# The first image's 3x3 convolution in pairs of rows, in a kernel of four layers (conv, scan, attention, filter)

## Chip, cores and metric

The kernel runs on one core of a Trainium2 chip. Its time is the device time of one execution in microseconds (us). The engines are TensorE (PE in the profile; its weight loads are PEld), VectorE (DVE), ScalarE (ACT), GpSimd (POOL) and SyncE (SP), whose queue issues all the DMAs here.

## What is computed

The input is x, four images of 64 x 64 points with 96 channels, in float32. Only the first part of layer 0 matters for the change:

```python
xz = x @ W_in.T                       # after a group norm of x
xp, z = xz[..., :192], xz[..., 192:]
xc = conv_general_dilated(xp, conv_w, (1, 1), [(1, 1), (1, 1)])   # 3x3, 192 -> 192
xc = silu(xc + conv_b)
x_dbl = xc @ x_proj_w.T               # 6 rows for delta, 16 for B, 16 for C
delta = softplus(dts @ dt_proj_w.T + dt_proj_b)
y = selective_scan(xc, delta, A, B, C)   # along rows and along columns, both ways
x = x + (y * silu(z)) @ W_out.T
```

Layer 1 (a depthwise 3x3 and a 1x1 convolution), layer 2 (linear attention and a quantised feed-forward) and layer 3 (an FFT filter and a second feed-forward) follow. They and the scans are the same text in both kernels.

## The kernel before

**Tiling.** Channels lie on partitions, points along the free dimension. An image is 4096 points, cut into 8 blocks (NBLK) of 512 points (BLK), each of 8 rows of 64 (RPB, HW). The 192 convolution channels are split into 128 ("low") and 64 ("high").

**Stages.** The program has three parts. The *head* (lines 1651 to 1703) makes the scan inputs of image 0. The *scan stage* (lines 1709 to 1812) runs 4 x 2 x 24 scans of 128 x 4096 with the work of images 1 to 3 spread between them by a planner (`pieces`, line 1583, with a table of gains and costs in us per step); its order is written out by hand. The *tail* (from line 1817) finishes image 3. In the head a list scheduler of the framework fixes the order of the instructions on each engine; every engine then runs its own list in order, and semaphores stand where one engine needs another's result.

**The head, block by block.** `before_scans(0, ...)` (line 270) returns five generators, which yield to each other:
- `project` (line 296): a block of x with a halo row on each side is loaded (line 304), normalised by ACT (line 320), multiplied by w_in into four PSUM banks (`p_xp`, line 333, four products of 320 or 256 columns) and copied by ACT into padded tiles of 10 x 66 points. `low` gets 128 channels (line 341). `high` gets the other 64 twice: on partitions 0 to 63 (line 343), and moved up by one row on partitions 64 to 127 (line 346), so that one product of 128 partitions does two kernel rows. There are two pairs of padded tiles, used in turn, and a pair comes free when the block that reads it is convolved (line 312).
- `project_z` (line 357): two products for z (line 367) and two ACT copies (line 373).
- `convolve` (line 377): for each half `oc` of the output channels, 15 products of 512 columns are summed in one PSUM bank (line 390): nine for the taps on `low`, three for two kernel rows at once on `high`, three for the last kernel row on `high[:64]`. ACT adds the bias and writes `u` (line 402). `u` has two buffers; the buffer of block i is that of block i - 2, which must have been multiplied by POOL (line 492) and stored.
- `gates` (line 418): ACT applies Silu to u and z (lines 427, 428), PE makes the 38 rows of x_dbl (`p_xd`, line 442; copied at line 450) and delta before the softplus (`p_dt`, line 456); ACT does the softplus in six steps (lines 464 to 472). Silu and the exponential/logarithm lie in different activation tables.
- `scan_inputs` (line 475): POOL does four operations of 96 x 512 for each half (lines 484 to 492), and delta and du go to DRAM through SP.

`first_loads` (line 1680) loads the first scans' inputs back, a quarter of the image for every two blocks; `times_b` (line 1475) multiplies them on POOL; the scans are at lines 1741 and 1792. Two more generators run in the head: `constants` (line 661) loads and prepares the weights of the later layers on SP, DVE and ACT (among them `bn_var`, one row spread over 97 partitions, with a square root on ACT at line 679), and `group_norm` (line 231) takes the statistics of images 1 to 3 on DVE, through four places of the tile `side`.

**Weights.** `conv_w` is one tile of 128 x 15 x 192, loaded by one DMA at line 1661 (1440 KB) before the head begins. Images 1 to 3 use the same tile in the scan stage.

Of the kernel before, what the change touches and what calls it, by code (L numbers as in the profile page):

```python
# [19 lines left out]
HW = 64  # L20
L = HW * HW
C = 96
DI = 192
NS = 16
NG = DI // 8
RK = 6
BLK = 512
NBLK = L // BLK
RPB = BLK // HW
# [19 lines left out]
NEXT = "next"  # L49
# [24 lines left out]
def layers(ctx: ExitStack, tc: tile.TileContext, a: dict, out):  # L74
# [4 lines left out]
    nc = tc.nc  # L79
# [22 lines left out]
    x1 = dram("x1", [C, L])  # L102
# [32 lines left out]
    done = {}  # L135
# [49 lines left out]
    us, xps, xbs, szs, pads = {}, {}, {}, {}, {}  # L185
# [38 lines left out]
    def until(ready):  # L224
        while not ready():
            yield NEXT
# [4 lines left out]
    def group_norm(wk, take, images, ready):  # L231

        n = len(images)
        mv = ca.tile([C, n, 2], F32, tag=f"mv{n}", name="mv")
        held = []
        yield from until(ready)
        for k, b in enumerate(images):
            stats = wk.tile([C, NBLK, 6], F32, tag="stats", name="stats", bufs=2)
            for i in range(NBLK):
                at = i % 4 * BLK  # L240
                xs = side[:, at : at + BLK]
                nc.sync.dma_start(xs, a["xT"][:, b * L + i * BLK : b * L + (i + 1) * BLK])
# [24 lines left out]
        for k, b in enumerate(images):  # L267
            norm[b] = gn[:, :, k]

    def before_scans(b, wk, take, deep=1, prev=None):  # L270

        x = a["xT"][:, b * L : (b + 1) * L]

        _, w_in, w_twice, conv_w, xproj, dt_w = kept

        def count(stage):

            before = NBLK if prev is None else done[stage, prev]
            return done.get((stage, b), 0) + before - NBLK

        if id(wk) not in pads:


            pads[id(wk)] = [
                tuple(
                    wk.tile([128, RPB + 2, HW + 2], F32, tag=f"{t}{k}", name=t)
                    for t in ("low", "high")
                )
                for k in range(2)
            ]  # L290
            for t in (t for pair in pads[id(wk)] for t in pair):
                for col in (0, HW + 1):
                    nc.gpsimd.memset(t[:, :, col : col + 1], 0.0)
        padded = pads[id(wk)]

        def project():

            yield from until(lambda: b in norm and count("z") > -2)
            gn = norm[b]

            def load_x(i):
                _, lo, hi = rows_of(i)
                xb = wk.tile([C, RPB + 2, HW], F32, tag="xb", name="xb", bufs=2)
                nc.sync.dma_start(
                    xb[:, : hi - lo, :],
                    x[:, lo * HW : hi * HW].rearrange("p (r w) -> p r w", w=HW),
                )
                return xb, clock[0]

            nxt = load_x(0)  # L310
            for i in range(NBLK):
                yield from until(lambda: i - 2 < count("conv") and i - 2 < count("z"))
                r0, lo, hi = rows_of(i)
                n = hi - lo
                yield NEXT
                xb, since = nxt
                yield from steps_past(since, LANDING)
                yield (0, 0.9, 0, 0)
                xbs[b, i] = xb
                nc.scalar.activation(  # L320
                    xb[:, :n, :], xb[:, :n, :], AF.Identity, scale=gn[:, 0:1], bias=gn[:, 1:2]
                )
                low, high = xps[b, i] = padded[i % 2]
                if i == 0 or i == NBLK - 1:
                    edge = 0 if i == 0 else RPB + 1
                    nc.gpsimd.memset(low[:, edge, :], 0.0)
                    nc.gpsimd.memset(high[:64, edge, :], 0.0)
                at = lo - r0 + 1
                for c in range(2):
                    for ra, rb in ((0, 5), (5, n)):  # L330
                        p, give = yield from take("p_xp", 128, (rb - ra) * HW)
                        yield (0.8, 0, 0, 0)
                        nc.tensor.matmul(
                            p, lhsT=w_twice if c else w_in[:, :128], rhs=xb[:, ra:rb, :],
                            start=True, stop=True,
                        )
                        yield NEXT
                        yield (0, 0.84 if c else 0.42, 0, 0)
                        rows = p.rearrange("p (r w) -> p r w", w=HW)
                        if c == 0:  # L340
                            nc.scalar.copy(low[:, at + ra : at + rb, 1 : HW + 1], rows)
                        else:
                            nc.scalar.copy(high[:64, at + ra : at + rb, 1 : HW + 1], rows[:64])

                            ja, jb = max(at + ra - 1, 0), min(at + rb - 1, RPB)
# [31 lines left out]
        def convolve():  # L377
            for i in range(NBLK):
# [38 lines left out]

        def gates():

            for i in range(NBLK):  # L420
                yield from until(lambda: i < count("u") and i < count("z"))
                cols = slice(i * BLK, (i + 1) * BLK)
                u = us[b, i]
# [9 lines left out]
                px, give = yield from take("p_xd", RK + 2 * NS)  # L433
# [3 lines left out]
                for c in range(2):  # L437
                    ud = k2("ud")
                    nc.scalar.mul(ud, u[:, c, :], d4[:, c : c + 1])
                    store(ud_s[b][c * C : (c + 1) * C, cols], ud)  # L440
                for c in range(2):
                    nc.tensor.matmul(
                        px, lhsT=xproj[:, c, :], rhs=u[:, c, :], start=(c == 0), stop=(c == 1)
# [2 lines left out]
                done["gate", b] = i + 1  # L446
                yield (1, 0.57, 0, 0, 1.6)
                flush()
                xd = wk.tile([RK + 2 * NS, BLK], F32, tag="xd", name="xd")
# [46 lines left out]
                flush()  # L496
                done["back", b] = i + c

        return [scan_inputs(), gates(), convolve(), project_z(), project()]


    def post(place, take, b, ahead, halves=(0, 1)):
# [935 lines left out]
    while len(delta_places) <= N:  # L1438
        p = delta_places[-1]
# [216 lines left out]
    for k in range(2):  # L1656
# [173 lines left out]
def host_layout(i):  # L1830
# [12 lines left out]
    for k in range(2):  # L1843
        o["convT"][k * 64 : k * 64 + 64, 9:12] = w[k, :, 128:].transpose(1, 0, 2)
    o["convT"][:64, 12:] = w[2, :, 128:].transpose(1, 0, 2)
    o["conv_b"] = cols(i["L0_conv_conv_b"], 2)
    o["xprojT"] = f(i["L0_conv_x_proj_w"].reshape(RK + 2 * NS, 2, C).transpose(2, 1, 0))
    o["dt_wT"] = f(i["L0_conv_dt_proj_w"].T)
# [89 lines left out]
```

## Time and profile before

| | us |
|---|---|
| median of 3 runs | 5845.36 (5842.83 to 5846.34) |
| the profiled execution: its time | 5842.19 |
| its span | 5840.4 |
| first and last convolution product of image 0 | 28.14, 317.7 |
| first scan | 347.21 |
| first scan of the last quarter (needs blocks 6 and 7) | 363.13 |

Busy shares of the span: PE 72%, DVE 82%, ACT 52%, POOL 76%. The profile's lists give for each group the line, the engine, what is written and read, the shape, the count, the busy time and the mean of one in ns, and the idle time ahead of it with what ended it. The timeline gives the start, the time from the first start to the last end of a run of like instructions, and the idle time ahead in brackets. A float32 matrix product stands as two records (the nine products on `low` are "x18"). Records overlap: the pace is the distance of starts, not the length of one.

### The profile page before, as it was taken

What the parts mean: (1) busy time and instruction counts of PE and PEld (TensorE: products, weight loads), DVE (VectorE), ACT (ScalarE), POOL (GpSimd) and SP (SyncE); (2) the same over time, 40 slices, a digit from 0 to 9 for tenths busy, and PEclk for the clock granted to TensorE, in tenths of its full rate; (3) what the DMA queues carried; (4) which work ended last, traced back from release to release, by engine and by line L of the source; (5) the groups of instructions that cost most, each with busy time, mean ns of one, the idle gap of its engine ahead of it and who ended that gap; (6) DMA issues with size and microseconds to landing.
All of it is one profiled execution on the core that took longest, in us unless ns stands there. A gap on an engine that the chain in (4) does not pass through costs nothing. (4 is left out here: it accounts for less than half of the span.)

```text
span 5840.4 us, 64640 instructions
## 1 busy us (share of the span) xinstructions
PE 4230.1 (72%) x19658; PEld 1612.3 (28%) x19658; DVE 4797.6 (82%) x3478; ACT 3044.6 (52%) x4205; POOL 4416.6 (76%) x2151
## 2 busy tenths in 40 slices
PE   8978888878973776664566776667678667667888
PEld 3322222222210221241331121245222114323345
DVE  2058898888899898998799999999999999979364
ACT  4667766766563346545454446444444554434233
POOL 1268888888889788888778989888898898867200
PEclk9979888888876776676777876668678767777888
DMA  3258878876698888788988867679887578886013
GB/s 105 80 163 233 234 215 225 242 221 195 187 253 237 222 216 223 206 243 237 246 240 224 228 185 211 194 212 249 230 235 206 164 210 235 245 230 191 22 39 104
DMA packets 469673, 1173.30 MB, mean 201 GB/s; under 512 B 90720, under 2 KB 155852, under 8 KB 469196
## 3 DMA queue, kind: packets, MB, share of 16 engines
q1 hardware_dynamic: 469324, 1169.17, 73.1%
q8 instruction: 156, 2.56, 0.2%
q14 instruction: 193, 1.58, 0.1%
HBM read 1012.05 MB, written 156.76 MB: 200 GB/s over the span
## 5 line engine op out<-in xcount | busy, mean ns | idle before, releaser
L1482 POOL TENSOR_TENSOR S<-S,rep 128x1024 f32<-128x1024 f32 x768 | 1807.6, 2356 | 541.5 <-DVE S L1802 485.4
L1495 ACT ACTIVATE pa<-dl,nega 128x1024 f32<-128x1024 f32 x1152 | 1285.3, 1117 | 1441.8 <-DVE S L1802 1076.0
L1478 POOL TENSOR_TENSOR B<-B,rep 128x1024 f32<-128x1024 f32 x768 | 1798.6, 2357 | 128.6 <-DMA B<-du_s 76.7
L1741 DVE TENSOR_TENSOR_SCAN S<-pa,S,B 128x1024 f32<-128x1024 f32 x576 | 1352.1, 2347 | 316.2 <-ACT pa L1495 128.6
L1509 PE MATMUL py<-S,red 128*32 128x512 f32 x3072 | 905.5, 845 | 739.9 <-POOL S L1482 491.4
L1792 DVE TENSOR_TENSOR_SCAN pa<-pa,edge,B 128x1024 f32<-128x1024 f32 x438 | 1029.7, 2351 | 46.3 <-ACT pa L1495 46.2
L1802 DVE TENSOR_TENSOR S<-S,pa 128x1024 f32<-128x1024 f32 x630 | 763.3, 1212 | 1.9
L1741 DVE TENSOR_TENSOR_SCAN S<-pa,B 128x1024 f32<-128x1024 f32 x192 | 436.4, 2273 | 189.5 <-ACT pa L1495 179.3
L390 PE MATMUL p_conv<-low,conv_w 128*96 128x512 f32 x1152 | 569.2, 647 | 8.7 <-ACT u L402 5.4
L1509 PEld LDWEIGHTS py<-S,red 128*32 128x32 f32 x3072 | 110.0, 125 | 1227.5 <-POOL S L1482 694.0
L1792 DVE TENSOR_TENSOR_SCAN pa<-pa,B 128x1024 f32<-128x1024 f32 x192 | 440.8, 2296 | 5.4
L154 ACT COPY side<-side 96x256 f32<-96x256 f32 (+1 forms) x448 | 278.9, 629 | 177.9 <-DMA deltaT_s<-side 74.5
L390 PE MATMUL p_conv<-high,conv_w 128*96 128x512 f32 (+1 forms) x768 | 356.6, 602 | 0.0
L1792 DVE TENSOR_TENSOR_SCAN dl<-pa,edge,B 128x1024 f32<-128x1024 f32 x138 | 323.1, 2341 | 16.3 <-ACT pa L1495 16.3
L1487 POOL TENSOR_TENSOR dl<-dl,rep 128x1024 f32<-128x1024 f32 x138 | 325.7, 2360 | 0.1
L1083 POOL CAST h<-y 128x1536 fp8e5<-128x1536 f16 x64 | 95.6, 1493 | 303.9 <-ACT y L794 286.3
L390 PEld LDWEIGHTS p_conv<-low,conv_w 128*96 128x96 f32 x1152 | 198.4, 179 | 390.8 <-issue 364.0
L905 PE MATMUL p_mean<-t,centre 96*96 96x512 f32 x256 | 174.8, 795 | 97.6 <-ACT sq L897 45.0
L1509 PE MATMUL py<-dl,red 128*32 128x512 f32 x552 | 219.2, 715 | 22.4 <-POOL dl L1487 22.3
L555 PE MATMUL p_y<-side,ident 96*96 96x512 f32 x336 | 207.1, 764 | 37.0 <-DVE q L948 11.6
L1517 ACT COPY ys<-py 128x512 f32<-128x512 f32 x384 | 221.9, 578 | 19.6 <-PE py L1509 18.2
L861 PE MATMUL p_l<-x,taps 96*96 96x504 f32 (+3 forms) x432 | 205.7, 629 | 16.4 <-DMA x<-x 12.5
(224 smaller groups left out, 5741.0 us busy)
## 6 DMA issues: line engine op xcount, KB each, us to landing
B<-du_s SPq DMA_DIRECT2D x768, 256.0 KB
dl<-delta_s SPq DMA_DIRECT2D x768, 256.0 KB
B<-duT_s SPq DMA_DIRECT2D x768, 256.0 KB
dl<-deltaT_s SPq DMA_DIRECT2D x768, 256.0 KB
z_s<-z SPq DMA_DIRECT2D x48, 512.0 KB
zl<-z_s SPq DMA_DIRECT2D x64, 384.0 KB
side<-y_s SPq DMA_DIRECT2D x120, 192.0 KB
rep<-bc_s SPq DMA_DIRECT2D x64, 256.0 KB
```

Source lines behind the costliest of these rows:

```text
L154: nc.scalar.copy(o.rearrange("p (w h) -> p w h", h=HW), t[:n, :].rearrange("p (h w) -> p w h", w=HW)[:, q * w : (q + 1) * w, :],)
L390: nc.tensor.matmul(p, lhsT=conv_w[: src.shape[0], k, oc * C : (oc + 1) * C], rhs=src[:, ky : ky + RPB, kx : kx + HW], start=(k == 0), stop ...
L555: nc.tensor.matmul(p, lhsT=ident[:C, :C], rhs=x, start=(j == 0), stop=(j == 2))
L1478: nc.gpsimd.tensor_tensor(Bs[n, q], Bs[n, q], reps[n // NG, 0, q], ALU.mult)
L1482: nc.gpsimd.tensor_tensor(Ss[n, q], Ss[n, q], reps[n // NG, 1, q], ALU.mult)
L1487: nc.gpsimd.tensor_tensor(dls[n, 0], dls[n, 0], reps[n // NG, 1, 0], ALU.mult)
L1495: nc.scalar.activation(pa, dls[n, q], AF.Exp, scale=nega[:, g : g + 1])
L1509: nc.tensor.matmul(py[32 * j : 32 * j + 32, :], lhsT=red, rhs=x[:, k * BLK : (k + 1) * BLK], start=(i == 0), stop=(i == len(terms) - 1),)
L1517: nc.scalar.copy(ys, pys.pop((n, half)))
L1741: nc.vector.tensor_tensor_scan(s, pas[q], Bs[n, q], Ss[n, q - 1][:, CH - 1 : CH] if q else 0.0, ALU.mult, ALU.add,)
L1792: nc.vector.tensor_tensor_scan(to[:, ::-1], pas[q][:, ::-1], Bs[n, q][:, ::-1], edge if k else 0.0, ALU.mult, ALU.add,)
L1802: nc.vector.tensor_tensor(Ss[n, q], Ss[n, q], to, ALU.add)
```

## The change

For image 0 alone (`b == 0`) the convolution is made in pairs of output rows. For an output pair (y0, y1) from four input rows d0 to d3 and three kernel rows k0, k1, k2, DVE makes d0 - d2, d1 + d2, d2 - d1 and d1 - d3 of every pair of rows in a block, for `low` and for `high` (eight operations of 128 x 264 for each block). PE multiplies them with k0, (k0 + k1 + k2)/2, (k0 - k1 + k2)/2 and k2, giving m0 to m3, and y0 = m0 + m1 + m2, y1 = m1 - m2 - m3. A product covers 4 x 64 = 256 columns; each of the four needs five (three column taps on `low`, one on `high` with two column taps stacked on the partitions, one on `high[:64]`), for both halves of the output channels: 40 products for a block in place of 30 of 512 columns. ACT writes m1 plus the bias to the odd rows of `u`, and DVE does four operations of 96 x 256 for each half to sum up. m0 and m1 share one bank, m2 and m3 another.

What goes with it: image 0 has one pair of padded tiles in place of two, free again once DVE has read it; `high` holds the second copy moved by a column instead of a row; the kernel rows come in as three DMAs (`convR`, 480 KB each), the combined ones are made by four DVE operations of 128 x 960; the usual `conv_w` is loaded at the end of image 0's convolution; for space, `group_norm` uses three places of `side` for images 1 to 3, and `xd` and one of two `ud` move into `side`.

```diff
-                at = i % 4 * BLK
+                at = i % (4 if n == 1 else 3) * BLK
...
+        pairs = b == 0
...
-                for k in range(2)
+                for k in range(1 if pairs else 2)
...
-                yield from until(lambda: i - 2 < count("conv") and i - 2 < count("z"))
+                yield from until(
+                    lambda: i - len(padded) < count("conv") and i - 2 < count("z")
+                )
...
+                            if pairs:
+                                nc.scalar.copy(
+                                    high[64:, at + ra : at + rb, :HW], rows[64:]
+                                )
+                                give()
+                                continue
...
+        def convolve_pairs():
+            last = wk.tile([128, 5, DI], F32, tag="last", name="last")
+            g = [conv_w[:, 5 * k : 5 * k + 5, :] for k in range(3)] + [last]
+            for k, t in ((0, g[0]), (2, last), (1, g[1])):
+                nc.sync.dma_start(t, a["convR"][:, k])
+            nc.vector.tensor_tensor(g[2], g[0], last, ALU.add)
+            nc.vector.tensor_scalar(g[1], g[1], 0.5, None, ALU.mult)
+            nc.vector.scalar_tensor_tensor(g[2], g[2], 0.5, g[1], ALU.mult, ALU.subtract)
+            nc.vector.scalar_tensor_tensor(g[1], g[1], 2.0, g[2], ALU.mult, ALU.add)
+            for i in range(NBLK):
+                yield from until(lambda: i < count("project"))
+                ds = []
+                for name, t in zip(("low", "high"), xps.pop((b, i))):
+                    at = [
+                        t[:, o : o + RPB, :].rearrange("p (j r) w -> p j r w", r=2) for o in (0, 2)
+                    ]
+                    d0, d1, d2, d3 = (at[k // 2][:, :, k % 2, :] for k in range(4))
+                    ds.append([])
+                    for k, (x0, x1, op) in enumerate(
+                        (
+                            (d0, d2, ALU.subtract), (d1, d2, ALU.add), (d2, d1, ALU.subtract),
+                            (d1, d3, ALU.subtract),
+                        )
+                    ):
+                        v = wk.tile([128, RPB // 2, HW + 2], F32, tag=f"{name}_v{k}", name="v")
+                        nc.vector.tensor_tensor(v, x0, x1, op)
+                        ds[-1].append(v)
+                done["conv", b] = i + 1
+                yield NEXT
+                ps, gives = {}, {}
+                for k in range(4):
+                    for oc in range(2):
+                        if k % 2 == 0:
+                            p, gives[oc] = yield from take("p_conv")
+                            ps[oc] = p.rearrange("p (m j w) -> p m j w", m=2, w=HW)
+                        low, high = (x[k] for x in ds)
+                        for j, rhs in enumerate(
+                            [low[:, :, kx : kx + HW] for kx in range(3)]
+                            + [high[:, :, :HW], high[:64, :, 2:]]
+                        ):
+                            nc.tensor.matmul(
+                                ps[oc][:, k % 2], lhsT=g[k][: rhs.shape[0], j, oc * C : (oc + 1) * C],
+                                rhs=rhs, start=(j == 0), stop=(j == 4),
+                            )
...
+                        if k == 1:
+                            nc.scalar.activation(
+                                odd, m1, AF.Identity, bias=conv_b[:, oc : oc + 1]
+                            )
+                            nc.vector.tensor_tensor(even, odd, m0, ALU.add)
+                        else:
+                            nc.vector.tensor_tensor(even, even, m0, ALU.add)
+                            nc.vector.tensor_tensor(odd, odd, m0, ALU.subtract)
+                            nc.vector.tensor_tensor(odd, odd, m1, ALU.subtract)
+                        gives[oc]()
+                done["u", b] = i + 1
+            for _ in range(4):
+                yield NEXT
+            nc.sync.dma_start(conv_w, a["convT"])
...
-        return [scan_inputs(), gates(), convolve(), project_z(), project()]
+        conv = convolve_pairs() if pairs else convolve()
+        return [scan_inputs(), gates(), conv, project_z(), project()]
...
-        const("conv_w", [128, 15, DI], a["convT"], wk),
+        wk.tile([128, 15, DI], F32, tag="conv_w", name="conv_w"),
```

More of the change, by code (lines that the diff above doesn't have):

```diff
@@ L293, in before_scans @@
                     nc.gpsimd.memset(t[:, :, col : col + 1], 0.0)
+            if pairs:
+                nc.gpsimd.memset(pads[id(wk)][0][1][64:, :, HW : HW + 1], 0.0)
         padded = pads[id(wk)]
@@ L322, in project @@
                 )
-                low, high = xps[b, i] = padded[i % 2]
+                low, high = xps[b, i] = padded[i % len(padded)]
                 if i == 0 or i == NBLK - 1:
@@ L326, in project @@
                     nc.gpsimd.memset(low[:, edge, :], 0.0)
-                    nc.gpsimd.memset(high[:64, edge, :], 0.0)
+                    nc.gpsimd.memset(high[: 128 if pairs else 64, edge, :], 0.0)
                 at = lo - r0 + 1
@@ L343, in project @@
                             nc.scalar.copy(high[:64, at + ra : at + rb, 1 : HW + 1], rows[:64])
+                            if pairs:
+                                nc.scalar.copy(
[3 more added lines that the diff above has]
+                                continue
                             ja, jb = max(at + ra - 1, 0), min(at + rb - 1, RPB)
@@ L406, in convolve @@
                 done["u", b] = i + 1
-        def k2(name, rows=C):
+        def convolve_pairs():
[42 more added lines that the diff above has]
+                            )
+                        if k == 0 and oc == 0:
+                            yield from until(lambda: i - 2 < count("back"))
+                            u = us[b, i] = wk.tile([C, 2, BLK], F32, tag="u", name="u", bufs=2)
+                        if k % 2 == 0:
+                            continue
+                        yield NEXT
+                        rows = u[:, oc, :].rearrange("p (j r w) -> p j r w", r=2, w=HW)
+                        even, odd = rows[:, :, 0, :], rows[:, :, 1, :]
+                        m0, m1 = ps[oc][:, 0], ps[oc][:, 1]
+                        if k == 1:
[10 more added lines that the diff above has]
+            for _ in range(4):
+                yield NEXT
+            nc.sync.dma_start(conv_w, a["convT"])
@@ L409, in k2 @@
+        def k2(name, rows=C):
+            if b == 0 and name == "ud":
+                flips[name] = flips.get(name, 0) ^ 1
+                if flips[name]:
+                    return side[:rows, 8 * BLK : 9 * BLK]
+                return wk.tile([rows, BLK], F32, tag=name, name=name)
             if b == 0 and name in ("w", "lg"):
@@ L448, in gates @@
                 flush()
-                xd = wk.tile([RK + 2 * NS, BLK], F32, tag="xd", name="xd")
+                if b == 0:
+                    xd = side[: RK + 2 * NS, 3 * BLK : 4 * BLK]
+                else:
+                    xd = wk.tile([RK + 2 * NS, BLK], F32, tag="xd", name="xd")
                 nc.scalar.copy(xd, px)
@@ L1845, in host_layout @@
     o["convT"][:64, 12:] = w[2, :, 128:].transpose(1, 0, 2)
+    o["convR"] = np.zeros((128, 3, 5, DI), np.float32)
+    o["convR"][:, :, :3] = w[:, :, :128].transpose(2, 0, 1, 3)
+    for k in range(2):
+        o["convR"][k * 64 : k * 64 + 64, :, 3] = w[:, k, 128:].transpose(1, 0, 2)
+    o["convR"][:64, :, 4] = w[:, 2, 128:].transpose(1, 0, 2)
     o["conv_b"] = cols(i["L0_conv_conv_b"], 2)
```

## The prediction

> **What bounds the kernel now.** I read first the busy times in three stretches, then the timeline of PE through the head, then that of all engines from the end of the convolution to the scans. In the first view the columns after the stretch are PE, PEld, DVE, ACT, POOL busy, the granted clock, the DMA share and GB/s.
>
> ```profile
> 25.00:318.00 293.00, 278.55 (x622) 100.72 (x621) 25.91 (x76) 174.49 (x241) 67.78 (x53) 0.95 0.31 90
> 318.00:363.10 45.10, 11.09 (x20) 2.60 (x18) 6.99 (x3) 30.71 (x42) 22.30 (x19) 0.59 0.43 117
> ```
>
> In the head PE is busy 278.55 of 293 us; DVE has 267 us free. Nothing of the scan stage runs before the head ends, and its order is fixed by hand (after the head the lists of both kernels agree on PE, ACT, DVE and POOL), so what the head loses or gains I carry one to one to the end.
>
> ```profile
> 56.97 7.89 PE L390 MATMUL p_conv<-low,conv_w 128*96 128x512 f32 x18
> 64.70 5.48 PE L390 MATMUL p_conv<-high,conv_w 128*96 128x512 f32 x12
> 70.11 0.81 PE L333 MATMUL p_xp<-xb,w_in 96*128 96x320 f32 x2
> ...
> 107.77 1.44 PE L333 MATMUL p_xp<-xb,w_in 96*128 96x320 f32 x2 [3.35 <-ACT xb L320]
> 109.00 8.99 PE L390 MATMUL p_conv<-low,conv_w 128*96 128x512 f32 x18
> ```
>
> From 56.97 to 70.11 one half of one block goes through without a gap. Once per block PE then waits about 3 us for ACT's `xb`, and the same product takes 1.44 us in place of 0.81, the next 18 records 8.99 in place of 7.89: the clock has dropped. From the 130.76 to the 209.33 start of two blocks' convolutions it is 39.3 us per block.
>
> ```profile
> 317.73 1.91 PE L442 MATMUL p_xd<-u,xproj 96*38 96x512 f32 x4
> 360.75 2.34 POOL L1478 TENSOR_TENSOR B<-B,rep 128x1024 f32<-128x1024 f32 x1 [6.03 <-DMA B<-du_s]
> 363.13 2.35 DVE L1741 TENSOR_TENSOR_SCAN S<-pa,S,B 128x1024 f32<-128x1024 f32 x1 [8.55 <-POOL B L1478]
> ```
>
> The head's end for the scans is 363.13: the last quarter waits for blocks 6 and 7, 45.4 us after the last convolution product, through ACT, POOL, a store and a load.
>
> [...] The trace has 357 ns at N=192 (line 743)[...] and 671 to 684 at 512[...]; I use it for 264 and 256 elements. [...] `bn_var` and its three kin have 97 partitions[...]: a DMA share of 0.07 is 1.1 of 16 engines, for some 12 us:
>
> ```profile
> 40.00:42.00 2.00, 2.00 (x7) 0.76 (x6) 0.00 (x0) 0.00 (x0) 0.00 (x0) 1.00 0.07 22
> 51.10 0.26 DVE L678 TENSOR_SCALAR bn_var<-bn_var 97x192 f32<-97x192 f32 x1 [15.24 <-DMA bn_var<-in_bn_var]
> ```
>
> **The change, part by part.**
>
> *Products.* Before: 13.14 us for each of 16 half blocks, 210 us. After: 320 products of 256 columns. No convolution of this width is in the trace; two records of a 256-column product of `p_xp` are, with their successor's start:
>
> ```profile
> 26.31 0.60 PE L333 MATMUL p_xp<-xb,w_twice 96*128 96x256 f32 x2
> 26.74 1.02 PE L367 MATMUL p_z<-xb,w_in 96*96 96x512 f32 x2
> ```
>
> 0.43 us for both, so for one product. Below, half of a 512-column product (7.73/9/2 = 0.43) is the floor; above, 0.53 if 0.05 us of each record's weight load (0.16) shows. I take 0.43: 138 us, or 17.2 per block for 26.3. At 0.53 it would be 32 us more.
>
> *A block on PE.* p_xp 2.65, p_xd 1.84, p_z 1.89, p_dt 1.88 (distances of starts, 123.23 to 130.76): 8.3. Before 34.6 of 39.3 us is work, the rest the wait and the slow clock. After: 17.2 + 8.3 + 0.5 for five more changes of operand at about 0.1 us = 26.0.
>
> *VectorE.* Per block eight operations at 0.43 and eight at 0.42: 6.8 us, beside products. What isn't hidden is the hand-over between blocks. The one padded pair lets the next projection start early, but in the order of the changed kernel the second pair of `p_xp` products and the copies to `high` come after the block's last product, then DVE's `high` differences, then the fourth product of the next block. PE has p_xp, p_dt, p_z (5.3 us), six `low` products (2.6) and mostly p_xd (1.8) to fill this. ACT needs 1 us for the first product, 0.85 for two copies, and between the copies sometimes a table load, Silu, a table load and half a softplus: 8.9 us in all, plus 0.4 on DVE. Mostly even; I put 1 us per block on it, for small waits. If the cover of p_z and p_xd were gone, 4 us more.
>
> *ACT.* The lists have 56 table loads before and 39 after, at 1.283 us: 22 us less; the 16 half-width writes save 16 x 0.3 = 5. A block on ACT is then 19 to 25 us: under PE's 26, but in block 5 all loads stay. There the chain from the first `high` copy to the next `xb` adds up to 22 us plus 1 to begin, while PE gets to its use in 18.7: 4.5 us of waiting and 2 to 3 of slow clock. I take 33 us for it.
>
> *The start.* The combined weights come in behind `nega` and ahead of `xb` on SP. Before, `nega` itself waited for the 1440 KB of `conv_w` (issue at 8.46, `nega` at 17.62), so that wait is only moved: three DMAs at about 14, 9.2 us for all, and `xb` behind them lands at 23.5 in place of 20.9. DVE's four preparations (1.16 us each) end by 26 under the projection. First product at 30.5 for 28.1. Bounds 28 to 34.
>
> *Blocks 0 and 1.* Block 0 now ends at 50. But ACT's in-order list has the square root of `bn_var` ahead of the copies for block 1, and DVE has that chain ahead of block 1's differences. Before, this was hidden: PE was busy until 57. `bn_var` is the last of the four on its one engine; SP now comes to them 1 to 2 us later. I take 53 for 51.1 (51 to 57). Then root 0.4, reciprocal 1.35 and small work to 56, table load and copies to 59.5, DVE's sums, statistics and differences to 63.3. Block 1 starts in effect at 61.6, and at 64 with the clock restored. So block 0's saving is lost and 7 us with it.
>
> *Sum of the head.* Block 1 from 64: 26 + 3 for its first softplus on ACT = 93; block 2, 28, = 121; blocks 3 and 4, 27 each, = 175; block 5, 33, = 208; block 6, 27, = 235; block 7 (no p_xp, p_z and p_dt ahead of its end), 20, = 255. Before: 317.7. So 63 us earlier.
>
> *After it.* ACT does nearly the same; half-width write, p_xd and softplus of block 6, Silu, softplus of block 7. Walking its list gives 47 us for 45.4. The reload of `conv_w` (1440 KB, 9.2 us) goes out on SP after block 6's `bc_s`; queued behind it are the first loads of the next scan and block 6's stores. It lands some 8 us before block 7's first store, which hides it; without this cover up to 9 us. `group_norm` with three places, and `xd` and `ud` in `side`, only make SP wait for DVE's statistics in blocks 1 and 2; every xb there still lands ahead of its use by 3 us or more. Zero, 5 us if not. POOL's memsets for block 7 wait for DVE ahead of block 4's operations: POOL works 10 of 27 us, zero.
>
> 302 for 363.13: 61 us. I take off 4 for clock drops after short waits[...]. **57 us**: the profiled execution 5842.2 - 57 = 5785, its span 5783; the median 5845.4 - 57 = 5788.
>
> **The rivals.**
> - *All covered:* `bn_var` lands in time and no block waits for ACT. 7 us in block 1, 3 in its softplus, 7 in block 5 and 2 elsewhere come back: 76 us, 5769. For it: 22 us less on ACT. Against: ACT and DVE run lists in order with the constants in them.
> - *Hand-overs bind everywhere:* every block from 1 to 6 runs like block 5. 64 + 6 x 33 + 20 = 282, + 47 = 329: 34 us[...], 5815. For it: each difference waits for ACT, each sum for PE, all on one in-order DVE. Against: only half the blocks have the table loads there.
> - *The clock (slower):* waits between blocks put PE at half clock for a large share h of the head. From 64 on its work is 6 x 26 + 20 = 176 us at full clock, with 20 us of waits: the end is 64 + 176(1 + h) + 20, and it passes 317.7 from h = 0.33; at h = 0.6 it is 366, which gives 5893. For it: the clock drops after waits of 1.8 and 3 us already. Against: the mean of 0.95 before is h = 0.1 with a 3 us wait per block.
> - *It doesn't reach the end:* another wait takes over the scans' start. 363.13 follows from POOL, DMA and ACT after the last product, all of block 7; nothing else is that late. Within 12 us: little.
>
> **How the numbers follow.** Forecast 0.55, all covered 0.18, hand-overs 0.17, the clock 0.06, no effect 0.04. A measurement of this kernel tells some 0.2%, 12 us, from no change. Faster 0.9, same 0.04, slower 0.06. The range goes from just past the first rival (5766) to past the second (5822), which also holds the price of `bn_var` at 57 and half of that of 0.53 us products; the rest is left out.
>
> **What would show it.** 256-column products 0.43 us apart; a gap of PE near 50 to 60 ended by DVE or ACT after `bn_var`; blocks of 26 to 28 us with one of 33; 39 table loads in the head; the last convolution product near 255; a scan of the last quarter near 302, then the same distance to the end as before (5477 us). Wrong would be a pace over 0.5, a block over 33 throughout, or a scan stage of another length.

## Result and the profile after

| | before | after |
|---|---|---|
| median, us | 5845.36 (5840.3 to 5861.85, 7 runs) | 5801.65 (5779.16 to 5815.78, 7 runs) |
| the profiled execution: its time, its span | 5842.19, 5840.4 | 5791.5, 5789.7 |
| first and last convolution product of image 0 (starts) | 28.14, 317.2 | 27.16, 265.8 |
| first scan of the last quarter | 363.13 | 307.25 |
| from there to the end of the span | 5477.3 | 5482.5 |

The changed kernel takes 0.992 of the time before (95% interval 0.9903 to 0.9938). The medians are 43.7 us apart, the profiled executions 50.7; the head itself is 55.9 us shorter. (The 317.7 of the table before the change is where the last product ended; its start, at 317.2, is the counterpart of 265.8.)

First the busy times by stretch, in the columns used before the change (PE, PEld, DVE, ACT, POOL, granted clock, DMA share, GB/s): from 25 to the last convolution product, and from there to the scan of the last quarter.

```profile
25.00:266.20 241.20, 232.50 (x784) 119.96 (x782) 78.63 (x196) 154.14 (x226) 68.90 (x53) 0.93 0.36 104
266.20:307.25 41.05, 11.99 (x16) 2.67 (x16) 8.74 (x9) 25.75 (x38) 23.13 (x26) 0.53 0.63 195
```

The head is still PE's: busy 232.5 of 241.2 us, for 278.55 of 293 before. VectorE has gone from 26 to 79 us. Now PE's timeline where block 0 ends, in block 1 and at the start of block 2 (start, length of the run of like records, idle time ahead):

```profile
48.37 1.34 PE L339 MATMUL p_xp<-xb,w_twice 96*128 96x320 f32 x4
54.94 5.68 PE L463 MATMUL p_conv<-v,conv_w 128*96 128x256 f32 x12 [5.23 <-DVE v L448]
...
72.92 5.06 PE L463 MATMUL p_conv<-v,conv_w 128*96 128x256 f32 x20
77.91 2.57 PE L463 MATMUL p_conv<-v,last 128*96 128x256 f32 x10
...
92.42 7.75 PE L463 MATMUL p_conv<-v,conv_w 128*96 128x256 f32 x19 [3.00 <-DVE v L448]
```

Three things stand in it. Block 1 waits 5.23 us for a difference of VectorE. Its first 12 records then take 5.68 us, where ten take 2.57 further down: the clock is halved (the granted clock is 0.50 from 53.9 to 64.1). And twenty records, which are ten products, start at 72.92 and their successor at 77.91: 4.99 us, 0.50 for each product, not 0.43. What ended block 1's wait is seen on the other engines in the same stretch:

```profile
48.77 0.26 DVE L770 TENSOR_SCALAR bn_var<-bn_var 97x192 f32<-97x192 f32 x1 [10.50 <-DMA bn_var<-in_bn_var]
49.07 0.36 ACT L771 ACTIVATE bn_var<-bn_var 97x192 f32<-97x192 f32 x1 [9.20 <-DVE bn_var L770]
...
52.90 0.43 ACT L347 COPY low<-p_xp 128x320 f32<-128x320 f32 x1
```

VectorE stands idle for 10.5 us until `bn_var` lands, ScalarE for 9.2 us ahead of the root, and only then comes the copy to `low` that block 1 needs; PE had made its operand by 46.1.

The blocks' first products come at 27.2, 54.9, 87.5, 121.8, 152.8, 185.4, 214.6 and 243.7. The end of the way to the scans:

```profile
277.56 3.63 PE L530 MATMUL p_xd<-u,xproj 96*38 96x512 f32 x4 [6.73 <-ACT u L515]
304.06 2.34 POOL L1570 TENSOR_TENSOR B<-B,rep 128x1024 f32<-128x1024 f32 x1 [5.64 <-DMA B<-du_s]
306.04 1.12 ACT L1587 ACTIVATE pa<-dl,nega 128x1024 f32<-128x1024 f32 x1 [11.75 <-DMA dl<-delta_s]
307.25 2.35 DVE L1833 TENSOR_TENSOR_SCAN S<-pa,S,B 128x1024 f32<-128x1024 f32 x1 [9.11 <-ACT pa L1587]
```

It is the same chain as before (p_xd, softplus, store, load, multiplication), 41.4 us long from the start of the last product for 45.9.

### The profile page after: what moved, and what is told of

It is laid out like the page before. It is cut to its first block, busy times and chain, and to the rows that moved or that the text cites. A ratio compares the mean times of both kernels' runs of the same rounds, so it can differ in the third digit from the quotient of the medians.

```text
span 5789.7 us, 65093 instructions
## 1 busy us (share of the span) xinstructions
PE 4187.2 (72%) x19818; PEld 1630.1 (28%) x19818; DVE 4858.5 (84%) x3610; ACT 3020.1 (52%) x4188; POOL 4417.0 (76%) x2148
## 3 DMA queue, kind: packets, MB, share of 16 engines
q8 instruction: 157, 2.57, 0.2%
## 5 line engine op out<-in xcount | busy, mean ns | idle before, releaser
L1574 POOL TENSOR_TENSOR S<-S,rep 128x1024 f32<-128x1024 f32 x768 | 1807.2, 2356 | 546.2 <-DVE S L1894 495.1
L402 PE MATMUL p_conv<-low,conv_w 128*96 128x512 f32 x864 | 437.4, 658 | 14.1 <-ACT u L414 9.6
L402 PE MATMUL p_conv<-high,conv_w 64*96 64x512 f32 (+1 forms) x576 | 269.7, 605 | 0.0
L402 PEld LDWEIGHTS p_conv<-low,conv_w 128*96 128x96 f32 x864 | 149.5, 181 | 319.0 <-issue 289.8
```

The lines of the kernel that those rows point to most:

```text
L402: nc.tensor.matmul(p, lhsT=conv_w[: src.shape[0], k, oc * C : (oc + 1) * C], rhs=src[:, ky : ky + RPB, kx : kx + HW], start=(k == 0), stop ...
L1574: nc.gpsimd.tensor_tensor(Ss[n, q], Ss[n, q], reps[n // NG, 1, q], ALU.mult)
```

## The experiments

The ratios stand against runs of the kernel before on the same chip; in brackets is their 95% interval. The scans' start (of the last quarter) and the start of the last convolution product are read in each one's single profile; "stage" is from that scan to the end of the span.

| kernel | last product | scans | stage | median, us | ratio (95%) |
|---|---|---|---|---|---|
| changed kernel again | 268.8 | 309.9 | 5496.4 | 5794.0 | 0.9927 (0.991 to 0.9945) |
| wide (fifth product on 128 partitions) | 245.0 | 288.8 | 5479.6 | 5773.4 | 0.9883 (0.9864 to 0.9902) |
| grouped (products on 64 partitions side by side) | 251.6 | 292.7 | 5488.8 | 5771.3 | 0.9877 (0.9857 to 0.9896) |
| bn_split (loads of `bn_var` and its kin split) | 248.4 | 289.9 | 5476.0 | 5780.7 | 0.99 (0.9881 to 0.9919) |
| late3 (later layers' constants two blocks later) | 251.5 | 293.0 | 5489.1 | 5776.8 | 0.9878 (0.9861 to 0.9896) |
| wide_bn (wide and bn_split) | 232.7 | 274.3 | 5510.7 | 5775.6 | 0.9875 (0.9854 to 0.9896) |
| wide_bn again | 232.1 | 276.1 | 5503.4 | 5769.5 | 0.9873 (0.9858 to 0.9889) |
| wide_late3 (wide and late3) | 237.2 | 279.6 | 5498.3 | 5779.7 | 0.9882 (0.9862 to 0.9902) |
| no_reload (usual `conv_w` not loaded) | 263.9 | 306.1 | 5482.2 | 5790.1 (1 run) | |
| twice (every product made twice) | 416.6 | 457.9 | 5486.5 | 5953.6 | 1.0187 (1.0173 to 1.0201) |
| diffs_twice (every difference made twice) | 275.1 | 315.7 | 5460.7 | 5794.8 | 0.9921 (0.9905 to 0.9938) |
| before, bn_split | 314.4 (its end) | 359.7 | 5495.1 | 5845.4 | 0.9996 (0.9986 to 1.0005) |

### Where the 0.50 us of a product comes from: wide, grouped

```diff
-                            + [high[:, :, :HW], high[:64, :, 2:]]
+                            + [high[:, :, :HW], high[:, :, 2:]]
```

> The fifth product of each set takes all 128 partitions of high (the weights' other 64 rows are zero), so that no product follows one of another number of partitions. Theory A: the pace of 0.50 us comes from the change between 64 and 128 partitions (0.17 us each, twice per five products). Five products then take 2.16 us in place of 2.50, a block's forty 17.3 in place of 20, and the head's last product comes 8 x 2.7 = 22 us earlier, near 244 if nothing else steps in; a wait for ScalarE may take back up to half: 11 to 22 us off the end. Rival B: the pace is that of reading 4 x 64 points with gaps, or of 256-column weights loads: still 0.50, no gain over 2 us.

```diff
-                        for j, rhs in enumerate(
+                        for j, rhs in list(enumerate(
...
-                        ):
+                        ))[:: 1 - 2 * oc]:
...
-                                rhs=rhs, start=(j == 0), stop=(j == 4),
+                                rhs=rhs, start=(j == 4 * oc), stop=(j == 4 - 4 * oc),
```

> The five products of the second half of the channels are taken in reverse order, so that two products on 64 partitions stand side by side: half the changes between 64 and 128 partitions, the same number of products of each kind. Theory A (the change of partitions costs, 0.17 us each): ten products take 4.66 us in place of 5.00, half of what the run with all on 128 partitions gains, some 11 us at the last product. Rival C (a product on 64 partitions is slow itself, 0.6 us for 0.43): no gain over 2 us here, though the run with all on 128 gains 22. Rival B: neither gains.

Ten products, and the start of what follows, in wide:

```profile
68.94 4.56 PE L463 MATMUL p_conv<-v,conv_w 128*96 128x256 f32 x20
73.34 2.32 PE L463 MATMUL p_conv<-v,last 128*96 128x256 f32 x10
```

and in grouped:

```profile
38.03 4.82 PE L463 MATMUL p_conv<-v,conv_w 128*96 128x256 f32 x20
42.69 2.49 PE L463 MATMUL p_conv<-v,last 128*96 128x256 f32 x10
```

4.40 us with every product on 128 partitions, 4.66 with half the changes, 4.99 as the kernel is. So it is the change that costs, not the 64-partition product as such (rival C: as many of them in grouped) and not the 256 columns (rival B). The last product is 20.8 us earlier in wide, where 22 were expected, and 14.3 in grouped, where 11 were; the profiles of the changed kernel scatter by 5 us there (263.9 to 268.8, no_reload counted with them).

These two differences hold more than the pace. Taking PE's idle time, and half of its busy time at half clock, off the way from the first product to the last leaves its work at full clock. That is 213.9, 214.1 and 214.2 us in the changed kernel (twice profiled) and in no_reload, so the 5 us of scatter lie in waits and clock. It is 193.5 us in wide and 206.3 in grouped: the pace gave 20.4 and 7.6 us. In wide, 8.0 us more of waiting (block 1 waits 8.26 us there) and 7.5 less of half clock nearly cancel; in grouped 9.5 of the 14.3 us are less half clock.

What happens at a change shows in the weight loads of the changed kernel, which have their own rows:

```profile
191.34 0.24 PEld L463 LDWEIGHTS p_conv<-v,conv_w 64*96 64x96 f32 x2 [0.36 <-issue]
191.94 0.24 PEld L463 LDWEIGHTS p_conv<-v,conv_w 128*96 128x96 f32 x2 [0.36 <-issue]
192.54 0.24 PEld L463 LDWEIGHTS p_conv<-v,conv_w 64*96 64x96 f32 x2 [0.36 <-issue]
193.14 1.54 PEld L463 LDWEIGHTS p_conv<-v,conv_w 128*96 128x96 f32 x8 [0.36 <-issue]
```

The eight loads of four like products follow each other in 1.54 us, while each change of partitions has 0.36 us of idle time ahead of the first load. A lone product from one change to the next then takes 0.60 us (191.34 to 191.94), 0.17 over 0.43; over the 128 changes of the head the 20.4 us make 0.16 each. In wide the twenty loads of the same products stand as one piece:

```profile
68.94 4.13 PEld L463 LDWEIGHTS p_conv<-v,conv_w 128*96 128x96 f32 x20 [0.78 <-issue]
```

Between these like products the loads run beside the records: 4.13 us of loads, and 4.40 us of twenty records, 0.22 for each. That a change from 128 to 64 partitions ends this (0.36 us of idle time, 0.60 us for the product) is what these two runs show; what in PE brings it about they don't.

With a pace of 0.43 us, another wait of the prediction is there. In wide, block 5:

```profile
184.88 1.11 PE L339 MATMUL p_xp<-xb,w_in 96*128 96x320 f32 x2 [4.12 <-ACT xb L326]
```

### Block 1's stall: bn_split, late3, and the same split in the kernel before

```diff
-            nc.sync.dma_start(t, a[f"bn1_{k}"].broadcast_to([C + 1, DI]))
+            nc.sync.dma_start(t[:C, :], a[f"bn1_{k}"].broadcast_to([C, DI])); nc.sync.dma_start(t[C:, :], a[f"bn1_{k}"])
```

> The four loads of 97 partitions (bn_gamma, bn_beta, bn_mean, bn_var) are each split into 96 and 1. Theory A: the second block's late start (54.9, after a gap of 5.2 us and then 10 us at half clock) is bn_var's landing at 48.8, on one DMA engine, with a square root in ScalarE's list ahead of the copies: bn_var then lands near 42, the gap goes, the second block starts near 50.5 and without the half clock: 7 to 10 us off the last product (266). Rival: the copies to low and high are late anyway (table loads, Silu of the block before): the block starts at 53 or later, gain under 3 us.

The timeline of bn_split at the same place:

```profile
39.46 0.26 DVE L770 TENSOR_SCALAR bn_var<-bn_var 97x192 f32<-97x192 f32 x1 [1.31 <-DMA bn_var<-in_bn_var]
...
48.24 1.34 PE L339 MATMUL p_xp<-xb,w_twice 96*128 96x320 f32 x4
...
49.42 7.49 PE L463 MATMUL p_conv<-v,conv_w 128*96 128x256 f32 x30
...
80.05 4.16 PE L463 MATMUL p_conv<-v,conv_w 128*96 128x256 f32 x15 [0.61 <-DVE v L448]
```

In the changed kernel the four loads, 72.8 KB each, went out from 32.7 to 37.0; from 34 to 46 the DMA share is 0.07, 1.1 of 16 engines, at 22 GB/s, and at this rate their 291 KB take 13 us. The split loads land at 39.5 in place of 48.8, block 1 starts at 49.42 without a wait and at full clock, and the wait inside block 2 shrinks from 3.00 to 0.61 us. The last product is 17.5 us earlier, some twice the 7 to 10 of theory A, with the scatter of 5 us above. 6.9 of them are less waiting (5.23 us in block 1 and 2.39 in block 2, less 0.69 of a new wait), and 10.9 less half clock while PE works, of which the spells from 53.9 to 64.1 and from 91.4 to 98.2 behind the two waits make 7.5: what followed these two stalls cost as much as the stalls. PE's work is the same (214.4 us for 213.9).

```diff
-    streams.append(constants(wk, take, blocks_done(1)))
+    streams.append(constants(wk, take, blocks_done(3)))
```

> The later layers' constants are let in two blocks later (the change counts a block as convolved when its differences are made, a block's products earlier than before), so that bn_var's root stands in ScalarE's list behind the copies of block 1. Theory A: what costs is where the root stands, not only the one-engine load: the gap of 5.2 us and the 3.0 us one after it go, and the last product comes near 249, as with the split loads. Rival B: the stall only moves to block 2, or the later root of 96 x 1 brings table loads into a full list: 258 or later.

Here `bn_var` lands later still, at 58.2, with 4.22 us of waiting on ScalarE; but both copies to `low` for block 1 stand ahead of the root, and PE starts block 1 at 49.16. Last product 251.5, where 249 was expected: theory A, it is the place in the lists that costs and not the late landing alone. The edit moves the whole chain of `bn_var`, VectorE's part with the root, so that it doesn't tell ScalarE's list from VectorE's.

> The split loads of bn_var in the kernel before. Theory A: block 0 covers the stall there (PE works until 57, ScalarE's root is done by 52): last product still at 317.7, within 1.5 us, and the time unchanged within the scatter. Rival B: the loads hold up something else in the head too (SP, DVE): last product at 313 or earlier, which would make it no cost of the change.

The time is unchanged (0.9996). The head is 3.4 us shorter, though: 0.9 at the first product (27.24) and 5.0 of PE's waits, among them 3.35 us for `xb` that the kernel before has at 107.8, less 2.6 for more half clock. Neither theory's number (316.2 to 319.2, or 313 and under) is met, and the changed kernel's own scatter of 5 us is larger. By these profiles at the most 3.4 us of the 17.5 was there before the change.

### Both together: wide_bn, twice run, and wide_late3

> Both edits: the fifth product on 128 partitions and bn_var's four loads split into 96 and 1. Theory A: the two costs are apart (20.8 us and 17.5 us at the last product, alone), so it is near 228, the scan of the last quarter near 270, the time 5760 or so. Rival B: with PE 38 us ahead ScalarE's list becomes the bound: waits for xb and for the copies of 3 to 4 us in several blocks (one of 4.1 us stood in block 5 with the first edit alone), each with some us of half clock behind it: the last product at 235 or later.

> The kernel with both edits once more: its scan of the last quarter stood at 274.3, 15.6 us ahead of that with split loads alone, but its five times (median 5775.6) were no better. Theory A: scatter of the scan stage, whose length was 5476 to 5511 us over the profiles so far; with as many times again the mean over both goes down to 5765 or so, and the second profile's stage is under 5500. Rival B: the scan stage takes back what comes in this early: again 5775 or more, with a stage of 5500 or more.

> The fifth product on 128 partitions with the constants two blocks later: another kernel with a head about as short (last product near 234, the scan of the last quarter near 276). Theory A (a head's shift reaches the end, within the scatter): a mean of 276 + 5485 + 2 = 5763, within 8. Rival B (what comes in early is taken back): 5775 or more.

The last product is at 232.7 and 232.1, between theory A (228) and B (235): the two gains nearly add up, with waits of 2.4 and 4.1 us for ScalarE's `xb` in block 5. The scans start 31 to 33 us ahead of the changed kernel's. But the times follow only in small part. The means of all runs: 5775.5 for the four kernels with one edit (20 runs, scans at 291 on the mean), 5773.5 for the three runs of both edits (14, scans at 277). Of 14 us, 2 came through, or 6 when each is taken against the kernel before on its own chip, with a standard error of some 4. All of them have lower ratios than the changed kernel, 0.9873 to 0.99 for its 0.992 and 0.9927 (the interval of bn_split overlaps with its own); among themselves (medians 5769.5 to 5780.7) these runs don't rank them.

### Does the head's length reach the end: again, twice, no_reload, diffs_twice

> The changed kernel once more, for a second profile. The head should repeat to 1 us: first convolution product at 27.2, second block at 54.9, last product near 266, a scan of the last quarter at 307. Theory A: the 5 us by which the way from there to the end was longer than before (5482 for 5477) are scatter of the scan stage, and a second profile gives another length, 3 us or more away from 5482, with a lag against before that comes and goes along the stage. Rival B: they belong to the change (its weights' reload, buffers moved), and come back within 1 us, in the same places.

> Each set of five products is made twice (the second time starts the sum anew), so that the head is longer by nearly 320 x 0.5 = 160 us and the work after it is the same. Theory A: the scan stage does not depend on when it starts: from the scan of the last quarter to the end it is 5476 to 5500 us as in the other profiles, and the mean time is the head's scan plus 5487, within 8. Rival B: a share of the head's shift is taken back by the stage (some 6 of 55 us by the means so far, 10%): then the stage is some 15 us shorter than that, near 5470.

```diff
-                        for j, rhs in enumerate(
+                        for j, rhs in 2 * list(enumerate(
...
-                        ):
+                        )):
```

With every product made twice the scans start at 457.9, 149 us after those of the changed kernel (308.6 on the mean of two profiles). The mean time is 5952.8, 154 us over its 5798.6 (13 runs). The stage of 5486.5 is theory A's, and the mean time is at the edge of it (457.9 + 5487 + 8). So a longer head does reach the end whole, and the 10% of rival B is not there. From one profile to the next of the changed kernel the head repeats to 3 us (1 was expected) and the stage is 5482.5 and 5496.4 (theory A of again), and in the kernel before 5477.3 and, with the split loads in its head, 5495.1.

Two places make up a part of this; what is left of the stage without them is 4525 to 4556 us over the profiles (4536 and 4540 in the changed kernel, 4540 in the kernel before), and was not followed up. One is the last 450 us, after the last scan. PE's busy time and the half clock go with its length (kernel before; changed kernel, first and second profile; wide_bn again):

```profile
5391.60:5840.40 448.80, 366.68 (x3327) 204.57 (x3323) 212.39 (x309) 139.96 (x238) 64.58 (x48) 0.83 0.17 56
```
```profile
5341.63:5789.73 448.10, 365.63 (x3327) 203.31 (x3323) 212.82 (x309) 139.96 (x238) 63.78 (x48) 0.83 0.17 56
```
```profile
5348.36:5806.28 457.92, 376.70 (x3327) 212.15 (x3323) 212.04 (x309) 140.12 (x238) 64.43 (x48) 0.81 0.17 54
```
```profile
5316.72:5779.55 462.83, 378.49 (x3327) 213.14 (x3323) 211.72 (x309) 140.14 (x238) 65.17 (x48) 0.80 0.17 54
```

The same instructions take 448 to 463 us; the half clock fills 155.2, 151.1, 178.0 and 182.9 us of it, and half of the 27 to 32 us between the second and the last two, 13 to 16, is about what these are longer, 10 to 15. No edit varied the clock there, so this is an agreement of sizes. The other place is the stretch from the 193rd scan instruction to the 337th (of 1536, each 1024 columns), with the convolutions of images 2 and 3 beside the scans. In 11 of the 14 profiles it has one of two lengths: 488.3 to 488.4 us in the kernel before, grouped, bn_split, late3 and diffs_twice, 498.4 to 498.6 in the changed kernel both times, wide, wide_bn both times and wide_late3. Between them lie no_reload and twice (491.6 and 491.8) and the kernel before with split loads (495.1). Kernel before, then changed kernel:

```profile
996.13:1484.57 488.44, 401.69 (x955) 118.80 (x956) 423.15 (x271) 326.22 (x455) 418.96 (x217) 0.84 0.79 220
```
```profile
945.70:1444.29 498.59, 407.05 (x955) 119.65 (x956) 423.19 (x272) 326.67 (x455) 418.87 (x217) 0.82 0.78 216
```

Equal work on DVE, ACT and POOL, 17 us more of half clock on PE (176.6 for 159.5), and in the waits of the changed kernel 37.8 us of scans for ScalarE's `pa` for 28.7 before, and 11.7 for PE's `py` for 6.1. The profiles with the long stretch have 173 to 177 us of half clock in it, those with the short one 159 to 166; whether that is cause or effect isn't shown. The two profiles of the changed kernel agree here to 0.2 us, those of wide_bn too, which speaks for a property of the kernel rather than of the run; no kernel of the short kind was profiled twice. Of the head's 55.9 us the changed kernel lost 10 in this stretch both times, and of the 14 that both edits together should bring over bn_split, late3 and grouped, it is 10. What puts a kernel on the one or the other side is open: neither the start of the scans orders them (grouped at 292.7 is short, wide at 288.8 long) nor any one edit.

```diff
-            nc.sync.dma_start(conv_w, a["convT"])
+            pass
```

> The load of the usual conv_w at the end of image 0's convolution is left out (images 1 to 3 are then convolved with the combined rows, the work being the same). Theory A: these 1440 KB are hidden: from the last convolution product to the scan of the last quarter it is 41.2 us with and without it, within 1 us. Rival B: the stores and loads of blocks 6 and 7 wait behind it, and the way gets shorter by 3 to 9 us.

From the last product (263.9) to the scans (306.06) it is 42.1 us, 41.4 and 41.1 in the two profiles of the changed kernel. The way gets no shorter without it, so the reload is hidden: theory A.

```diff
-                        nc.vector.tensor_tensor(v, x0, x1, op)
+                        nc.vector.tensor_tensor(v, x0, x1, op); nc.vector.tensor_tensor(v, x0, x1, op)
```

> VectorE makes each of a block's eight differences twice, with the same result: 3.4 us more of VectorE in each block, 27 us in all. Theory A (the prediction's step: VectorE's work lies beside the products, only the hand-over between blocks is small waits): the last product within 5 us of the three profiles of the changed kernel so far (263.9 to 268.8), the time within the scatter. Rival B: the differences of high, on the way from the copies to the next block's fourth product, hold PE in every block: 1.5 to 3 us each, 12 to 24 us, a last product at 278 or later.

The last product is at 275.1: outside theory A's 273.8, short of B's 278. The waits say where the 9 us are:

```profile
58.33 4.13 PE L463 MATMUL p_conv<-v,conv_w 128*96 128x256 f32 x9 [8.90 <-DVE v L448]
```

This is block 1, 8.90 us for 5.23; inside block 2 it is 3.90 for 3.00, inside block 3 2.50 for 0.47: 6.6 us together. After that PE waits once, 0.63 us; more half clock (37.4 us of PE's work for 32.1) makes the rest. VectorE's work was hidden where PE was ahead, and added up with `bn_var`'s stall where PE was waiting anyway.

## Why the prediction came out as it did

The sum was right: 57 us forecast for the profiled execution, 50.7 measured there, 43.7 by the medians; 5801.65 lies in the range of 5766 to 5822. It is right in the head (55.9 us) partly because errors of both signs met.

- **The products' pace was mis-sized.** 0.43 us was taken from a pair of like products, with 0.53 as the bound; it is 0.50. The term that the working lacked is the change between 128 and 64 partitions: 0.17 us, twice in each set of five, 8 blocks x 8 sets x 0.34 = 22 us (wide: 20.4 of PE's work). Before there was one such stretch of three products in fifteen. By its own list ("wrong would be a pace over 0.5") it stood at the limit. A block is 29 to 34 us and not 26 to 28.
- **Block 5's 33 us did not come** (29.1, no wait for `xb`), because of that pace: PE was late enough for ScalarE. Once the products take 0.43 us, the wait is there, 4.12 us for 4.5 forecast. So this step was right at the pace that it assumed.
- **Block 1's stall was right in mechanism.** `bn_var` landed at 48.8 (forecast 53, bounds 51 to 57, so below them), the root held up the copies, the granted clock fell to 0.50 (from 53.9). Block 2 starts at 87.5 for 93. But the whole price is some 17.5 us by one profile of bn_split, not the 10 that the prediction gave back in its first rival (7, and 3 in block 1's softplus): block 2's wait and the half clock after it follow from it.
- **The start** came at 27.16, before the lower bound of 28 (forecast 30.5): the three loads of the kernel rows went out from 12.0 (forecast 14) and had all landed by 18.5, so that `xb` behind them was there at 19.4 and not at 23.5. This term was too large by 4 us.
- **The clock.** Half clock came without a wait of PE too: 6.8 us each from 149.5 and 180.2 and 3.4 us from 241.6, in stretches of `p_xp`, `p_dt` and `p_z` in which PE has no gap. The prediction counted it after waits alone (and gave it 4 us at the most). In the kernel before, five of the head's six spells of half clock (granted clock 0.50) begin in a wait of PE of 1.76 to 3.35 us or at its end, and two here go with the waits of 5.23 and 3.00 us; but ahead of these three, as ahead of the sixth one before the change, at 288.7, the records show no idle time. What stands there instead is `p_dt`, a product on 6 partitions; the four records of `p_z` behind it take 3.42 us up to the next product at 152.81, for the 1.89 that the prediction has for them:

```profile
146.32 1.09 PE L547 MATMUL p_dt<-side,dt_w 6*96 6x512 f32 x2
...
148.17 1.09 PE L547 MATMUL p_dt<-side,dt_w 6*96 6x512 f32 x2
...
149.39 3.63 PE L379 MATMUL p_z<-xb,w_in 96*96 96x512 f32 x4
```

The same shows in the heads of all 14 profiles, cut into 3.41 us from the edges of the half-clock spells, 909 stretches at full clock. An estimate of PE's use, made from the records of these traces, weights each record's time by its partitions over 128. Under 0.425 all 51 stretches were followed by half clock, over 0.515 none of 831, between them 9 of 27, with gaps in them or without. So half clock went with stretches in which this use is low, be it for idle time or for products on few partitions. That this is its cause is an estimate: no run varied `p_dt` to test it, and the two bounds are read off these same stretches.

- **ScalarE's table loads**: 39 ahead of the scans in place of 56, as forecast, at 1.283 us each; 12 of the 39 stand right ahead of a Silu (lines 515 and 516), 6 ahead of an exponential (line 559) and 6 ahead of a logarithm (line 562).
- **The tail** (from the end of the last product) is 41 us and not 47. Behind the last product ScalarE has two table loads in place of five, 3 x 1.28 = 3.8 us: block 6's softplus no longer alternates with block 7's.
- **Reload and VectorE's work hidden**: right (no_reload; diffs_twice outside the stalled blocks). 54 of the 64 differences took 0.41 to 0.44 us for 0.43 forecast, which lies on the line from 357 ns at 192 elements to 671 to 684 at 512. The other ten took 0.97 to 1.51 us, each with POOL at work at the same time, and 9.4 us more in all; the 64 sums, with one operand in PSUM, took 0.42 us at the most, seven of them with POOL at work too.
- **"Then the same distance to the end" was wrong** by 5.2 us in the profile. The stage's length goes with the half clock at its end and with the stretch above: this kernel took 10 us more in the stretch with the convolutions of images 2 and 3, and 5 less elsewhere. What sets either is open.

In sum: 5.5 us early at block 2 (3.3 of them from the start), 14 late from there to block 7 (156 us for 142) and 2.5 in block 7, both by the pace and the clock, 6 early in the tail. Of the rivals, "all covered" failed by `bn_var` and by the pace; "hand-overs bind everywhere" had the block lengths nearly right (29 to 34) for a wrong reason: PE, not ScalarE, was what they waited for. The clock was at half for some 34 us of the head, h = 0.14, far from the 0.33 at which the change would have lost.

## What to carry to other kernels

A product on 64 partitions among those on 128 was not cheaper here but dearer (0.60 us for 0.43): padding it with zero weights to the same partitions, or putting two such side by side, took 20 and 8 us off PE's work. When the engine that hides a stall gets faster, look in the in-order lists for what it hid: a constant's slow load and one square root cost some 17.5 us where they had cost 3 at the most. To read such runs, part the work at full clock from waits and half clock: the first repeated to 0.3 us where the last product scattered by 5. And carry a shift of the start to the end only as far as runs show it: 149 us more arrived whole, of 14 us less 2 to 6.

## What the hardware showed that was not expected

- A change from 128 to 64 partitions or back between float32 products of 256 columns cost 0.16 to 0.17 us (20.4 us over 128 changes in wide; 0.60 us for 0.43 in the changed kernel's weight loads).
- Half clock in stretches of PE without a gap, in multiples of 3.41 us (3.41 to 10.24 in the head), ahead of which products on 6 partitions ran for 1.0 to 2.05 of 3.41 us.
- A fixed sequence of 490 us with all engines waiting for each other took 488.3 to 488.4 us in five profiles, 498.4 to 498.6 in six and 491.6 to 495.1 in three; the two kernels profiled twice, both with the long one, repeated it to 0.2 us.
